# Two shared PSUM banks in turn, ScalarE's convolution steps spread out, and column sums with standing ones, in a selective-scan kernel

## The chip, the cores and the metric

The kernel runs on one core of a Trainium2 chip. The metric is the device time of one execution in microseconds (us). Each kernel was run several times in rounds, next to the kernel before on the same chip. All executions quoted here were in the fast state, and every kernel gave correct results. The kernel before had a median of 5537.85 us in the three runs that came with the case (5533.6 to 5543.78).

Names of engines: PE is TensorE, PEld its weight load, DVE is VectorE, ACT is ScalarE, POOL is GpSimd.

## The reference, cut to what matters

A binary-weight convolution block feeds a selective scan in four directions; layer norm, attention and a feed-forward layer follow. Nearly all of the time is the scan:

```python
delta = softplus(delta + delta_bias)
def step(h, inp):
    ut, dt, Bt, Ct = inp
    dA = exp(dt[..., None] * A[None])                       # decay
    h = dA * h + (dt * ut)[..., None] * Bt[:, :, None, :]   # scan
    y = einsum('bkdn,bkn->bkd', h, Ct)                      # product and sum over the state
    return (h, y)
```

There are 4 images, 4 directions, 4096 positions, 192 channels and a state of 16.

## The kernel before: the parts that matter

The scan is cut into 1536 pieces of 128 partitions by 1024 positions. Each piece needs these instructions:

- POOL "injects": `w <- dl * bc`.
- ACT makes the decay `dA` (an Exp) in one of two PSUM buffers of two banks each.
- DVE scans. Its result stays in the PSUM buffer (`dA`), or goes to SBUF (`h`) if POOL will take the product.
- DVE or POOL multiplies by C. The builder decides by running estimates: 940 products go to DVE, 596 to POOL.
- PE sums products into `yp`, a PSUM bank that holds eight pieces; ACT empties it (`ys`).
- ACT copies the last column as the carry (`cy`).

```python
for i in range(n):                     # one piece a step; cut
    if i >= 1: self.carry(i - 1)                       # ACT, one column
    if i % 8 == 3 and i > 8: self.evacuate(i - 4)      # ACT empties the bank of y
    if i + 1 < n: self.decay(i + 1)                    # ACT, Exp into a buffer "dA"
    if i >= 3: self.reduce(i - 3)                      # PE
    if i + AHEAD < n: self.inject(i + AHEAD)           # POOL
    self.late_product()                                # POOL, product of the piece before
    self.scan(i)                                       # DVE, and the product if it is DVE's
    if i % 8 == 0 and self.todo: lanes.append(self.prepare())   # delta, one tile in 8 pieces
    interleave(lanes)                                  # one step of delta
    next(back, None)                                   # one step of the "back" work
```

The "back" work is everything else (convolution, layer norms, attention, feed-forward), one step per piece. Delta is prepared in steps too; each `yield` ends a step:

```python
ps = p.ps.tile([128, 512], F32, tag="dps")             # delta's own PSUM bank
... 8 matmuls into ps ...;                         yield
ACT: Abs(ps) -> d;  ACT: Relu(ps) -> t;            yield
ACT: Exp(d) -> d;   ACT: Ln(d) -> ps;              yield
PE: ps += ident * t;                               yield
DVE: d[:, 1] = ps * u                              # "delta's product"
yield
ACT: d[:, 0] = copy(ps)                            # "delta's copy", pd <- dps
```

In the convolution, DVE forms `cz` in a PSUM bank, ACT takes its sign (`sg`) and then Exp, Ln and Exp for a SiLU, DVE makes `u` from `cz`, and ACT copies `u` by columns (`ut`) in the same step.

## Time and profile before

| What | Before | Where it is read |
|---|---|---|
| Span of the profiled run | 5538.9 us, clock 0.714 | cores |
| DVE, POOL busy | 5052.4 us, 4994.2 us (91%, 90%) | busy times |
| ACT, PE busy | 64%, 62% | busy times |
| DVE idle from 340 to 5410 us | 213 us | stretches |
| PE waits for ACT to empty y's bank | 621.9 us, 141 times | waits |
| ACT's delta copy waits for DVE | 3.7 us, once | groups |

A busy share says which engine can set the time, and its gaps say where. DVE and POOL are full; PE and ACT matter only where they make those two wait. The scans of the 1536 pieces run from about 269 to 5419 us. The lines themselves are in the prediction below.

The copy of delta is where the change bites, so here is its line in the groups of the kernel before (busy us, mean ns | idle of the engine just before it, and who ended it):

```profile
L1185 ACT COPY pd<-dps 128x512 f32<-128x512 f32 x189 | 109.2, 578 | 3.7 <-DVE pd L401 3.7
```

The 189 copies wait once, 3.7 us in all: DVE's product lies a whole step earlier.

### The profile page before, as it was taken

To read this page: it belongs to the slowest core of one execution; us is meant where nothing else is said; L and a number is where in the kernel's file an instruction comes from. 1 tells how busy PE (TensorE), PEld (TensorE's weight loads), DVE (VectorE), ACT (ScalarE), POOL (GpSimd) and SP (SyncE) were. 2 spreads that over 40 slices of the span, in tenths; PEclk is the share of its full clock that TensorE was granted. 3 is DMA by queue.
4 is the path that set the end of the run, shared out by engine and by line. 5 is a ranking of instruction groups with operands and counts; after the bars stand their busy time and mean duration, and the time that the engine had idled before them with its cause. 6 is when DMAs were issued, how large, how long until landed. Compare 5 with 4: busy or idle time off the path is not lost. (4 is left out here: it accounts for less than half of the span.)

```text
span 5538.9 us, 62371 instructions
## 1 busy us (share of the span) xinstructions
PE 3432.7 (62%) x20197; PEld 1356.7 (24%) x20197; DVE 5052.4 (91%) x3237; ACT 3556.7 (64%) x5564; POOL 4994.2 (90%) x2262
## 2 busy tenths in 40 slices
PE   6456665576557766577656766544676564444677
PEld 3222222222223222222222222211232121111223
DVE  3299999999999999899999999999999999999984
ACT  4467776777666667677766666755556775555554
POOL 2199999999999999899999999999999999999981
PEclk8667776678767876667777777766787766566778
DMA  4456666866766566666656566665666665665652
GB/s 78 118 179 198 207 194 193 258 193 199 220 203 194 194 205 199 218 217 207 205 193 212 185 200 210 212 211 191 210 215 186 191 205 198 205 208 190 207 159 60
DMA packets 613244, 1069.93 MB, mean 193 GB/s; under 512 B 225083, under 2 KB 343924, under 8 KB 611124
## 3 DMA queue, kind: packets, MB, share of 16 engines
q1 hardware_dynamic: 599428, 1065.88, 61.4%
q8 instruction: 159, 2.61, 0.2%
q10 hardware_dynamic: 13488, 0.07, 0.1%
q14 instruction: 169, 1.38, 0.1%
HBM read 833.20 MB, written 229.38 MB: 192 GB/s over the span
## 5 line engine op out<-in xcount | busy, mean ns | idle before, releaser
L401 POOL TENSOR_TENSOR w<-dl,bc 128x1024 f32<-128x1024 f32 x1536 | 3579.9, 2356 | 166.7 <-PE yp L1302 93.2
L1231 ACT ACTIVATE dA<-dl,anm 128x1024 f32<-128x1024 f32 x1536 | 1715.6, 1117 | 477.0 <-DVE w L401 291.5
L1302 PE MATMUL yp<-w,sum 128*32 128x256 f32 x12288 | 1261.6, 507 | 1083.2 <-ACT ys L1316 621.9
L401 DVE TENSOR_TENSOR_SCAN dA<-dA,cy,w 128x1024 f32<-128x1024 f32 x706 | 1654.4, 2343 | 94.7 <-ACT dA L1231 83.4
L401 POOL TENSOR_TENSOR w<-h,bc 128x1024 f32<-128x1024 f32 x596 | 1402.6, 2353 | 93.7 <-DVE h L401 85.2
L401 DVE TENSOR_TENSOR w<-dA,bc 128x1024 f32<-128x1024 f32 x940 | 1151.4, 1225 | 47.7 <-DVE dA L401 0.5
L401 DVE TENSOR_TENSOR_SCAN h<-dA,cy,w 128x1024 f32<-128x1024 f32 x446 | 1043.3, 2340 | 9.2 <-ACT dA L1231 8.7
L1302 PEld LDWEIGHTS yp<-w,sum 128*32 128x32 f32 x12288 | 308.0, 127 | 2136.9 <-issue 705.4
L1271 ACT COPY cy<-dA 128x1 f32<-128x1 f32 x707 | 110.8, 157 | 692.0 <-DVE w L401 690.7
L401 DVE TENSOR_TENSOR_SCAN dA<-dA,w 128x1024 f32<-128x1024 f32 x234 | 534.2, 2283 | 22.3 <-ACT dA L1231 18.0
L577 PE MATMUL cv<-tp,cw 96*96 96x512 fp8e5 x1152 | 359.9, 456 | 85.6 <-ACT r L627 70.5
L401 DVE TENSOR_TENSOR_SCAN h<-dA,w 128x1024 f32<-128x1024 f32 x150 | 341.8, 2279 | 24.4 <-POOL w L401 23.6
L1179 PE MATMUL dps<-sp,ident 128*128 128x512 f32 x378 | 356.8, 1043 | 0.0
L1307 PE MATMUL yp<-ya,back 128*128 128x256 f32 x576 | 237.8, 534 | 0.0
L577 PEld LDWEIGHTS <-cw 96*96 96x96 fp8e5 x1152 | 159.0, 146 | 277.5 <-issue 223.8
L1271 ACT COPY cy<-h 128x1 f32<-128x1 f32 x445 | 82.7, 186 | 145.6 <-DVE h L401 144.5
L847 PE MATMUL yc<-eys,mean 96*96 96x512 f32 x240 | 134.6, 713 | 33.3 <-DMA eys<-yd 14.5
L1307 PEld LDWEIGHTS yp<-ya,back 128*128 128x128 f32 x576 | 123.9, 248 | 127.8 <-issue 97.1
L1172 ACT ACTIVATE pd<-dps,dbias,pvd 128x512 f32<-128x512 f32 x189 | 143.8, 761 | 16.4 <-PE dps L1167 13.0
L1173 ACT ACTIVATE sp<-dps,dbias,pvd 128x512 f32<-128x512 f32 x189 | 144.7, 766 | 0.0
L401 DVE TENSOR_TENSOR pd<-dps,pu 128x512 f32<-128x512 f32 x189 | 127.6, 675 | 4.6 <-DMA dl<-dld 4.3
L1316 ACT COPY ys<-yp 128x512 f32<-128x512 f32 x192 | 111.7, 582 | 30.2 <-PE yp L1307 24.3
(282 smaller groups left out, 4017.6 us busy)
## 6 DMA issues: line engine op xcount, KB each, us to landing
dl<-dld SPq DMA_DIRECT2D x768, 512.0 KB
bc<-bcd SPq DMA_DIRECT2D x512, 512.0 KB
dld<-pd SPq DMA_DIRECT2D x126, 512.0 KB
yd<-ys SPq DMA_DIRECT2D x768, 64.0 KB
dld<-pd SPq DMA_DIRECT2D x126, 256.0 KB
ya<-yd SPq DMA_DIRECT2D x192, 128.0 KB
pu<-ud SPq DMA_DIRECT2D x32, 512.0 KB
pu<-utd SPq DMA_DIRECT2D x31, 512.0 KB
```

Source lines behind the costliest of these rows:

```text
L401: return getattr(self.eng, name)(out, *args, **kw)
L577: nc.tensor.matmul(ps, c.cw[:, j, t, 96 * h : 96 * h + 96], tpad[j][:, 8 * q + dy : 8 * q + dy + 8, dx : dx + IW], start=(j == 0 and t == ...
L847: self.c.nc.tensor.matmul(ps, w, x, start=(i == 0), stop=(i == len(pairs) - 1))
L1172: nc.scalar.activation(d[:, 0], ps, AF.Abs, scale=sc, bias=bi)
L1173: nc.scalar.activation(t, ps, AF.Relu, scale=sc, bias=bi)
L1179: nc.tensor.matmul(ps, c.ident, t, start=False, stop=True, skip_group_check=True)
L1231: c.nc.scalar.activation(t, self.dlt[i // NQ][0], AF.Exp, scale=c.anm[:, g, NQ * KORD[e] + q : NQ * KORD[e] + q + 1])
L1271: self.c.nc.scalar.copy(self.carries[g, q], h[:, CH - 1 : CH])
L1302: c.nc.tensor.matmul(y[32 * x : 32 * x + 32, g % 2, :], c.sum4, prod[:, 256 * x : 256 * x + 256], start=(q == 0), stop=(q == NQ - 1 and no ...
L1307: c.nc.tensor.matmul(y[:, g % 2, :], w, src, start=False, stop=(n == len(more) - 1))
L1316: c.nc.scalar.copy(t, y[:, :, ::-1] if k >= 2 else y)
```

## The change

The intent is to let PE start the sums of the next eight pieces while ACT still empties the last, and to even out ACT's load. The two PSUM banks that y and delta own become two banks that they use in turn, y in one and delta in the other, and they swap every eight pieces. For that, delta must be out of its bank earlier, so its copy moves into the step of DVE's product and delta starts at piece 4 of eight. The rest: the bank of y is emptied behind the decay; ACT's pairs of delta instructions are split; the store of delta is issued a step later; the sign goes to the step of `u`, `ut` a step behind `u`, and the convolution's 18 taps (its matmuls) are dealt 5, 5, 5, 3 to the steps; the column sums of x use the ones as the first, standing operand of the matmul, where x stood before; a fourth delta tile is made at the start. The diff is cut to the main lines (`...`).

```diff
-        ps = ... p.ps.tile([128, 512], F32, name=f"dps_{nm}", tag="dps")
+        ps = ... p.ps.tile([128, 512], F32, name=f"dps_{nm}", tag=f"y{1 - self.bank()}")
         nc.scalar.activation(d[:, 0], ps, AF.Abs, scale=sc, bias=bi)
+        yield
         nc.scalar.activation(t, ps, AF.Relu, scale=sc, bias=bi)
         yield
         nc.scalar.activation(d[:, 0], d[:, 0], AF.Exp, scale=-1.0)
+        yield
         nc.scalar.activation(ps, d[:, 0], AF.Ln, bias=1.0)
...
         c.vec.tensor_tensor(d[:, 1]..., ps..., uv, ALU.mult)
-        yield
         nc.scalar.copy(d[:, 0], ps)
...
-            self.ydone[i // 8] = c.p.ps.tile(..., name=f"yp_{i}", tag="y")
+            self.ydone[i // 8] = c.p.ps.tile(..., name=f"yp_{i}", tag=f"y{i // 8 % 2}")
...
+            if i + 1 < n:
+                self.decay(i + 1)
             if i % 8 == 3 and i > 8:
                 self.evacuate(i - 4)
-            if i + 1 < n:
-                self.decay(i + 1)
...
-            if i % 8 == 0 and self.todo:
+            if i % 8 == 4 and self.todo:
... (convolution, inside its steps s = 0..3)
+                    if s == 0 and turned:
+                        by_columns(*turned)          # ut, a step behind u
                         elif s == 1:
-                            ... AF.Sign of pz ...    # sg
                             nc.scalar.activation(e, pz, AF.Exp, scale=-1.0)
...
+                        elif s == 3:
+                            sign(ph, pq, pz)         # sg, now in the step of u
                             c.vec.tensor_tensor(u, pz, e, ALU.mult)
... (column sums, of 32 blocks of x)
-                nc.tensor.matmul(csum, xts[i // 8][:, i % 8, :], c.ones1, ...)
+                nc.tensor.matmul(csum, c.ones1, xts[i // 8][:, i % 8 : i % 8 + 4, :]..., ...)
```

More of the change, by code (lines that the diff above doesn't have):

```diff
@@ L188, in transposed @@
             count[0] += 1
-            ps = p.ps.tile([128, 1024], BF16, name=f"tps{count[0]}", tag=("y", "dps")[count[0] % 2])
+            ps = p.ps.tile([128, 1024], BF16, name=f"tps{count[0]}", tag=f"y{count[0] % 2}")
             at = 0
@@ L350, in weights @@
         )
-        ps = p.ps.tile([128, 512], F32, name="tpd", tag="dps")
+        ps = p.ps.tile([128, 512], F32, name="tpd", tag="y0")
         for g in range(3):
@@ L507, in prologue @@
                 yield
-            csum = bank("csum", 0)[0:96, 0:1]
-            for i in range(NT):
-                nc.tensor.matmul(csum, xts[i // 8][:, i % 8, :], c.ones1, start=(i == 0), stop=(i == NT - 1))
-                if i % 8 == 7:
-                    yield
+            csum = bank("csum", 0)[0:1, 0 : 4 * DM]
+            for i in range(0, NT, 4):
+                nc.tensor.matmul(
+                    csum, c.ones1, xts[i // 8][:, i % 8 : i % 8 + 4, :].rearrange("p i e -> p (i e)"),
+                    start=(i == 0), stop=(i == NT - 4),
+                )
+                if i % 8 == 4:
+                    yield
+            row = f32("csr")[0:1, 0 : 4 * DM]
+            nc.scalar.copy(row, csum)
+            ps = bank("cst", 1)[0:96, 0:1]
+            for i in range(4):
+                nc.tensor.matmul(
+                    ps, row[:, DM * i : DM * i + DM], c.ones1[0:1, :], start=(i == 0), stop=(i == 3)
+                )
+            yield
             cs = f32("cs")[0:96, 0:1]
-            nc.scalar.copy(cs, csum)
-            gsum = bank("gsum", 1)[0:96, 0:1]
+            nc.scalar.copy(cs, ps)
+            gsum = bank("gsum", 0)[0:96, 0:1]
             nc.tensor.matmul(gsum, c.grp, cs, start=True, stop=True)
@@ L563, in prologue, with by_columns, sign @@
             one = lambda h: slice(h, h + 1)
-            prev = None
+            prev = turned = None
             two = c.p.dA.tile([128, CH], F32, name=f"cv2_{b}", tag="dA") if alone else None
             utp = sub.enter_context(tc.tile_pool(name=f"ut_{b}", bufs=1))
+            uts = {}
+            def by_columns(h, q, u):
+                if q % 4 == 0:
+                    uts[h] = utp.tile([96, IW, 32], F32, name=f"ut{h}{q}_{b}", tag="ut")
+                ut, at = uts[h], 8 * (q % 4)
+                dst, src = ut[:, :, at : at + 8], u.rearrange("p (h w) -> p w h", w=IW)
+                (nc.gpsimd.tensor_copy if alone else nc.scalar.copy)(dst, src)
+                if q % 4 == 3:
+                    rows = slice(8 * q - 24, 8 * q + 8)
+                    c.later.store(c.utd[b][h].rearrange("p (w h) -> p w h", h=IH)[:, :, rows], ut, after=1)
+            def sign(h, q, pz):
+                sg = f32(f"sg{h}{q}")[0:96, 0:128]
+                nc.scalar.activation(
+                    sg.bitcast(F8).rearrange("p (h e i) -> p h e i", h=8, e=2),
+                    pz.rearrange("p (h i e) -> p h e i", h=8, e=2), AF.Sign, saturate=False,
+                )
+                for m in range(3):
+                    g0 = 64 * (m // 2) + 32 * h
+                    c.later.store(xgw[g0 : g0 + 32, m % 2, 128 * q : 128 * q + 128], sg[m::3, :])
             for n, part in enumerate(parts + [None]):
@@ L574, in prologue @@
                     if part:
-                        for j, t in taps[(0, 5, 9, 14)[s] : (5, 9, 14, 18)[s]]:
+                        for j, t in taps[5 * s : min(18, 5 * s + 5)]:
                             dy, dx = divmod(t, 3)
@@ L581, in prologue @@
                             )
+                    if s == 0 and turned:
+                        by_columns(*turned)
+                        turned = None
                     if prev:
@@ L587, in prologue @@
                         elif s == 1:
-                            sg = f32("sg" + pn)[0:96, 0:128]
-                            nc.scalar.activation(
-                                sg.bitcast(F8).rearrange("p (h e i) -> p h e i", h=8, e=2),
-                                pz.rearrange("p (h i e) -> p h e i", h=8, e=2), AF.Sign, saturate=False,
-                            )
-                            for m in range(3):
-                                g0 = 64 * (m // 2) + 32 * ph
-                                c.later.store(xgw[g0 : g0 + 32, m % 2, 128 * pq : 128 * pq + 128], sg[m::3, :])
+                            if alone:
+                                sign(ph, pq, pz)
                             e = f32("e" + pn)[0:96]
@@ L601, in prologue @@
                             nc.scalar.activation(e, e, AF.Exp, scale=-1.0)
-                        else:
+                        elif s == 3:
+                            if not alone:
+                                sign(ph, pq, pz)
                             u = f32("u" + pn)[0:96]
@@ L605, in prologue @@
                             c.later.store(c.ud[b][ph][:, 512 * pq : 512 * pq + 512], u)
-                            if pq % 4 == 0:
-                                ut = utp.tile([96, IW, 32], F32, name=f"ut{pn}_{b}", tag="ut")
-                            at = 8 * (pq % 4)
-                            dst, src = ut[:, :, at : at + 8], u.rearrange("p (h w) -> p w h", w=IW)
+                            turned = (ph, pq, u)
                             if alone:
-                                nc.gpsimd.tensor_copy(dst, src)
-                            else:
-                                nc.scalar.copy(dst, src)
-                            if pq % 4 == 3:
-                                rows = slice(8 * pq - 24, 8 * pq + 8)
-                                c.later.store(
-                                    c.utd[b][ph].rearrange("p (w h) -> p w h", h=IH)[:, :, rows], ut, after=1
-                                )
+                                by_columns(*turned)
+                                turned = None
                     yield
@@ L633, in prologue @@
                     yield
+            if turned:
+                by_columns(*turned)
             c.later.flush()
@@ L1119, in done, with bank @@
         return self.at > (b * NK + n) * NPC + SETTLE
+    def bank(self):
+        return max(0, self.at - 3) // 8 % 2
     def load_signs(self, b, k):
@@ L1161, in prepare @@
         d = spare[0] if spare else p.pd.tile([128, 2, 512], F32, name=f"pd_{nm}", tag="pd")
-        ps = spare[3] if spare else p.ps.tile([128, 512], F32, name=f"dps_{nm}", tag="dps")
+        ps = spare[3] if spare else p.ps.tile([128, 512], F32, name=f"dps_{nm}", tag=f"y{1 - self.bank()}")
         pv = ps.rearrange("p (c q s) -> p s q c", q=4, s=8)
@@ L1175, in prepare @@
         nc.scalar.activation(d[:, 0], d[:, 0], AF.Exp, scale=-1.0)
+        yield
         nc.scalar.activation(ps, d[:, 0], AF.Ln, bias=1.0)
@@ L1189, in prepare @@
             then = (lambda: self.loaded.add((b, k, ci, part))) if x == len(groups) - 1 else None
-            c.later.store(dst, d[r0 : r0 + n], after=1, then=then)
+            c.later.store(dst, d[r0 : r0 + n], after=2, then=then)
     def load_bc(self, w, to, b, e, ci, q):
@@ L1297, in reduce @@
         if i % 8 == 0:
-            self.ydone[i // 8] = c.p.ps.tile([128, 2, 256], F32, name=f"yp_{i}", tag="y")
+            self.ydone[i // 8] = c.p.ps.tile([128, 2, 256], F32, name=f"yp_{i}", tag=f"y{i // 8 % 2}")
         y, prod = self.ydone[i // 8], self.ins.pop(i)
@@ L1324, in run @@
         c, lanes, n = self.c, [], len(self.pieces)
-        w = [c.p.w.tile([128, CH], F32, name=f"w_s{x}", tag="w") for x in range(7)]
+        w = [c.p.w.tile([128, CH], F32, name=f"w_s{x}", tag="w") for x in range(8)]
         ps = [c.p.dA.tile([128, CH], F32, name=f"dA_s{x}", tag="dA") for x in range(2)]
@@ L1345, in run @@
             self.load_dl(m)
+        u = c.p.pu.tile([128, CH], F32, name="pu_s", tag="pu")
+        for _ in self.prepare((w[7].rearrange("p (t l) -> p t l", t=2), w[4][:, 512:CH], u, ps[1][:, 512:CH])):
+            pass
         self.decay(0)
```

## The prediction

> **What bounds the kernel now.** I read the busy times first, then busy time by stretches, then each engine's waits, then the instruction groups, and last the order of the built program.
>
> ```profile
> PE 3432.7 (62%) x20197; PEld 1356.7 (24%) x20197; DVE 5052.4 (91%) x3237; ACT 3556.7 (64%) x5564; POOL 4994.2 (90%) x2262
> 3700.00:3900.00 200.00, 97.83 (x635) 34.29 (x636) 197.48 (x115) 102.97 (x150) 196.92 (x86) 0.61 0.60 195
> 340.00:5410.00 5070.00, 3161.05 (x18864) 1214.60 (x18862) 4857.31 (x2969) 3334.33 (x5199) 4869.21 (x2120) 0.71 0.64 203
> ```
>
> The first line is the page's busy line; the others are stretches (start:end, length, busy time of PE, PEld, DVE, ACT, POOL with instruction counts, then clock and DMA). DVE and POOL share the work and are both nearly full from about 340 us, when the scans run steadily, to 5410 us. In these 5070 us DVE is idle 5070 - 4857 = 213 us and POOL 201 us. In the quietest stretch, where nothing but scans runs (3700 to 3900), DVE still idles 2.5 us of 200, or 1.3%. I take that as the floor of back-to-back issue: 1.3% of 5070 is 65 us. So at most 213 - 65, about 148 us or 2.7% of 5538, can come out of the steady part by any reordering, unless work is removed.
>
> ```profile
> L401 POOL TENSOR_TENSOR w<-dl,bc 128x1024 f32<-128x1024 f32 x1536 | 3579.9, 2356 | 166.7 <-PE yp L1302 93.2 <-DMA dl<-dld 62.8 <-DMA bc<-bcd 7.4
> L401 POOL TENSOR_TENSOR w<-h,bc 128x1024 f32<-128x1024 f32 x596 | 1402.6, 2353 | 93.7 <-DVE h L401 85.2 <-DMA x1b<-x1d 1.5 <-PE yp L1307 1.4
> L401 DVE TENSOR_TENSOR_SCAN dA<-dA,cy,w 128x1024 f32<-128x1024 f32 x706 | 1654.4, 2343 | 94.7 <-ACT dA L1231 83.4 <-ACT cy L1271 7.2 <-POOL w L401 2.7
> L1316 ACT COPY ys<-yp 128x512 f32<-128x512 f32 x192 | 111.7, 582 | 30.2 <-PE yp L1307 24.3 <-PE yp L1302 5.0 <-DMA dl<-dld 0.6
> ```
>
> These are groups: line, engine, operation, shapes, count, then busy us and mean ns of one, then idle before them and who ended it. None of POOL's 1536 + 596 multiplications goes away: in the order of the built programs POOL again has 1536 and 596, and DVE 1536 scans and 940 products. What can shrink is the right-hand column.
>
> ```profile
> PE yp L1302 <- ACT ys L1316: 621.9, 141, 10.8
> DVE dA L401 <- ACT dA L1231: 101.3, 86, 5.5
> POOL w L401 <- PE yp L1302: 93.6, 58, 8.6
> ACT ut L614 <- DVE u L401: 91.6, 45, 3.6
> DVE g L401 <- PE sy L847: 19.7, 9, 4.6
> ```
>
> In these lines of the waits (total, times, longest) the largest, 622 us, belongs to PE, which is 62% busy: it is the wait that two banks are to remove, but it counts only where it ends in one of the two small ones below it, PE making POOL wait (93.6) and ACT making DVE wait (101.3). The two small ones add, since DVE and POOL feed each other over a few buffers; POOL's 85 us on DVE's h are the echo of DVE's own stalls.
>
> **What the Trainium skill says.** "Perfetto Trace Analysis", Identifying the Most-Contended Engine, says to work on the engine with the highest occupancy and find what its gaps wait for. The trace agrees: PE's 622 us lie on an engine with room, DVE and POOL are the ones to look at. "PSUM — Partial Sum Buffer", PSUM bank collisions raise a hardware error, says two engines must not touch one bank in the same quadrant at once, reads against reads included, and that software has to keep them apart. The trace fits: ScalarE's one-column carry copy, which only needs the scan, mostly starts after DVE's product from the same tile (waits of ACT cy on DVE w: 690.7 us). [...]"ScalarE: Activation LUTs", Rules for kernel authors, budgets about 0.3 us per activation plus 0.83 ns per element, 0.73 us for 512. The trace has 0.58 to 0.77, so splitting ScalarE's steps moves work without making it cheaper.
>
> **Two banks in turn.** Before, y has one bank and delta the other. The first sum of an eight-piece block waits until ScalarE has emptied the bank. Afterwards it goes to the other bank; but delta now lives there for most of the block. In the built program the first sum of a block waits for ScalarE's copy of delta, which stands at the end of the step after DVE's delta product. Before: wait for scan (and product) of piece i+2, carry 0.16, copy 0.58. After: the same scan, delta product 0.68, copy 0.58, so about 0.5 us later. So the 622 us wait of PE is mostly not removed: it gets a new name. What improves is the tie to a late PE: the evacuation no longer stands between PE's last sum and its next, and the delta matmul that needs it comes two sums later. Of POOL's 93.6 us on PE, the five longest (8.6, 5.65, 5.12, 3.58, 3.02, sum 26) come after PE stood on a DMA (delta's signs, the x load of the column sums) and stay. Of the other 68, mostly in the epilogue where PE is 75% busy, I expect a third or so to go: -25 us.
>
> **Evacuation behind the decay.** ScalarE waited 24.3 + 5.0 us for PE in front of its evacuation, with the next decay behind it; and in about eight places delta's Exp and Ln, another pair and the evacuation lined up ahead of one decay, some 2 us late each. Not all of it reached DVE: -10 us.
>
> **Delta's copy in the same step as DVE's product.** ScalarE now stands on DVE at that place. Afterwards it has copy 0.5, up to 1.3 of other work, carry 0.1 and decay 1.05 before DVE's next scan but one; DVE has a scan of 2.29, and a product of 1.15 if it is its own. Walking the built order with these durations, 32 of the 188 places come late, 0.27 us each on average: +9 us.
>
> **Decays that wait for the scan right before their own.** In the built program most decays wait for the piece two back, but 73 of 1536 wait for the previous scan (on a tile whose product POOL takes); after the change it is 87. Each such decay (1.12 us) can't hide, and the trace shows DVE gaps of exactly 1.25 us, 48 us in 46 gaps over 0.3 us. 14 more, of which 46/73 count: 14 x 0.63 x 1.25 = +11 us.
>
> **Convolution, u a step behind.** ACT's 91.6 us on u go, but ACT has room there: between 1200 and 1400 us, a convolution, DVE is busy 98.63 and 97.03 of each 100 us, near the floor of 98.7. About 1 us per 100 over three convolutions of some 260 us: at most -6, say -5 us. ScalarE's total per part is unchanged.
>
> **Column sums.** Before, 32 matmuls (64 passes) with a weight load each, 10.3 us a batch at the start, 2.7 us a step later. After, 8 matmuls of 384 columns, 16 passes; the trace's 512-column fp32 passes take 0.56 to 1.04 us, so 384 take 0.4 to 0.8 by estimate, 7 to 12 us. A wash, plus one copy and four tiny matmuls. The stall there (DVE busy 89.00 of 100 at 1000 to 1100) starts with PE waiting for x from DMA and stays: -3 us in all.
>
> **Start.** A fourth delta tile is made before the first scan. ScalarE and PE have the time (they wait for dl until 264.9), but DVE's product needs a u load issued at 264.33 behind six dl loads; DMA is busy until about 273.7, and the first scan began at 268.96. Up to 5 us late, but POOL fills its six tiles until 280.4 and DVE waits 9.2 us for it anyway; and one delta step less at once. +2 us. The rest of the start and the tail are the same work.
>
> Sum: -25 - 10 + 9 + 11 - 5 - 3 + 2 = -21 us; 5538 - 21 = 5517 us.
>
> **Rivals.** First, PE's idle time is the real brake: epilogue and prologue matmuls stand in order behind the blocked sum, ScalarE stands behind them (sq on yc 78.5, fq on fc 42.4 us) and DVE behind ScalarE. For it: DVE is busy only 195.8 of the last 230 us before 5410. Against: much of that is PE's own load. It could bring 70 to 90 us: 5450 to 5470. Second, the new ties cost more than they free: the bank comes back only after DVE's delta product, so a late DVE blocks PE, PE blocks POOL, and ScalarE standing on DVE delays back work and decays. Against: POOL fills four pieces ahead with nine tiles, so a sum may be about two pieces (6.6 us) late. It could cost 30 to 50 us: 5570 to 5590. Third, all gaps of DMA origin stay and nothing moves: 5538.
>
> **Range and chances.** The terms are some 10 to 25 us each with the first the least sure. 5455 to 5570 holds both half-strength rivals. Faster by over 2% means below 5427, 111 of the 148 us that are there at all: 0.04. Slower by 2%, above 5648, would need a new stall at every block (0.6 us at each of 188): 0.03. Same: 0.93.
>
> **What would show it.** PE's wait for ACT ys nearly gone and a wait for ACT pd of a few hundred us in its place; POOL's wait on PE near 70; DVE's wait on ACT dA between 95 and 120; ACT's wait on u gone and one on DVE pd new; busy time of POOL and DVE unchanged. If POOL's wait on PE falls below 30 us, or DVE's wait on ACT rises above 150, I was wrong.

## The result, and the profile after

The changed kernel took 5578.6 us (median of four runs, 5574.11 to 5580.39) against 5539.91 us for the kernel before in the same rounds: 39 us slower. The ratio is 1.007, with a 95% interval of 1.0052 to 1.0087. Ratios here are the mean time of one kernel's fast runs over that of the other's of the same rounds, so not quite the ratio of the medians quoted. The prediction, 5517 us with a range of 5455 to 5570, had the sign wrong and missed the range. "Same within 2%" was right.

Busy times of the changed kernel, from its page, and then its stretches (start:end, length, busy time of PE, PEld, DVE, ACT, POOL with counts, clock, DMA share, GB/s):

```profile
PE 3522.2 (63%) x20037; PEld 1360.0 (24%) x20037; DVE 5054.6 (91%) x3237; ACT 3546.4 (64%) x5568; POOL 4995.2 (90%) x2262
```

```profile
3700.00:3900.00 200.00, 96.64 (x630) 33.25 (x630) 197.50 (x113) 104.01 (x152) 197.22 (x86) 0.65 0.58 190
340.00:5410.00 5070.00, 3217.35 (x18556) 1209.21 (x18556) 4830.94 (x2950) 3301.92 (x5171) 4845.72 (x2109) 0.70 0.64 202
```

DVE and POOL do the same work to within about 2 us. In the quiet stretch, where scans and delta run without back work, DVE is busy 197.50 us of 200, as before. In the long stretch its idle time rose from 213 to 239 us. So the loss is more waiting, and it lies where back work runs beside the scans and delta.

The groups of the changed kernel that answer to those shown of before, and the copy:

```profile
L401 POOL TENSOR_TENSOR w<-dl,bc 128x1024 f32<-128x1024 f32 x1536 | 3578.8, 2355 | 156.9 <-PE yp L1333 77.5 <-DMA dl<-dld 68.2 <-DMA bc<-bcd 5.8
L401 POOL TENSOR_TENSOR w<-h,bc 128x1024 f32<-128x1024 f32 x596 | 1402.3, 2353 | 137.3 <-DVE h L401 123.2 <-PE yp L1338 3.0 <-DMA yd<-ys 1.9
L401 DVE TENSOR_TENSOR_SCAN dA<-dA,cy,w 128x1024 f32<-128x1024 f32 x705 | 1651.8, 2343 | 94.0 <-ACT dA L1262 73.2 <-ACT cy L1302 8.8 <-POOL w L401 6.3
L1216 ACT COPY pd<-dps 128x512 f32<-128x512 f32 x188 | 110.0, 585 | 459.3 <-DVE pd L401 459.3
```

And its waits (who waits for whom: us in total, times, longest):

```profile
PE yp L1333 <- ACT pd L1216: 358.3, 104, 6.4
POOL w L401 <- PE yp L1333: 77.5, 48, 6.6
DVE dA L401 <- ACT dA L1262: 96.7, 80, 2.8
DVE u L401 <- ACT sg L594: 12.6, 14, 2.2
DVE dA L401 <- ACT cy L1302: 11.3, 8, 2.5
DVE pd L401 <- PE dps L1211: 10.2, 3, 7.5
```

Each line that the prediction named came about as named: the wait of PE is renamed from `ys` to `pd`; POOL's wait on PE fell from 93.6 to 77.5; DVE's wait on the decay, here 96.7, stayed in its band. The copy, which waited 3.7 us before, now stands 459.3 us on DVE (184 times), and this costs ACT nothing that its own busy time would show. By itself such a stand need not cost DVE anything. In the quiet stretch (3700 to 3900 us) the copy waits as well, in eight places, and DVE has no gap there that the waits show (over 0.15 us):

```profile
ACT pd L1216 <- DVE pd L401: 19.5, 8, 3.1
```

Elsewhere new small lines stand against DVE: 12.6 us on the sign, 10.2 us on delta's own matmul, more on carries.

To account for it, I summed DVE's gaps from the 32nd scan to the last in both traces. That stretch is 38.6 us longer after the change, and DVE's idle time in it grew by 36.5 us (212.4 to 248.9). By who ended the gap: sign +12.6, PE for delta's product +10.2, carries +5.4, PE for the attention sums (`vk`) +5.0, PE for the output (`op`) +4.3, decays +4.3, POOL +4.2, column sums +2.8; against these PE's `sy` -6.5 and a late DMA of delta's -4.3. Note how little of it is decays, 4.3 us, although the prediction's two terms on late decays came to 20; the evacuation, moved by the same change, may be one reason (experiment evac_only).

### The profile page after: what moved, and what is told of

It reads as the page before. It is cut to its first block, busy times and chain, and to the rows that moved or that the text cites. A ratio compares the mean times of both kernels' runs of the same rounds, so it can differ in the third digit from the quotient of the medians.

```text
span 5572.3 us, 61825 instructions
## 1 busy us (share of the span) xinstructions
PE 3522.2 (63%) x20037; PEld 1360.0 (24%) x20037; DVE 5054.6 (91%) x3237; ACT 3546.4 (64%) x5568; POOL 4995.2 (90%) x2262
## 5 line engine op out<-in xcount | busy, mean ns | idle before, releaser
L401 POOL TENSOR_TENSOR w<-dl,bc 128x1024 f32<-128x1024 f32 x1536 | 3578.8, 2355 | 156.9 <-PE yp L1333 77.5
L1333 PE MATMUL yp<-w,sum 128*32 128x256 f32 x12288 | 1328.6, 528 | 827.8 <-ACT pd L1216 358.3
L1216 ACT COPY pd<-dps 128x512 f32<-128x512 f32 x188 | 110.0, 585 | 459.3 <-DVE pd L401 459.3
L1338 PE MATMUL yp<-ya,back 128*128 128x256 f32 x576 | 216.4, 493 | 0.0
L1211 PEld LDWEIGHTS dps<-sp,ident 128*128 128x128 f32 x376 | 85.9, 284 | 384.8 <-ACT dps L1208 325.6
L1197 PE MATMUL dps<-gT,wdz 128*128 128x64 fp8e5 x1000 | 119.8, 323 | 37.9 <-DMA gT<-gTd 20.0
```

Source lines behind the costliest of these rows:

```text
L401: return getattr(self.eng, name)(out, *args, **kw)
L1197: nc.tensor.matmul(pv[:, s], wd[:, k, s], gT[:, :, c0 : c0 + 16], start=(s == 0), stop=(s == 7))
L1211: nc.tensor.matmul(ps, c.ident, t, start=False, stop=True, skip_group_check=True)
L1216: nc.scalar.copy(d[:, 0], ps)
L1333: c.nc.tensor.matmul(y[32 * x : 32 * x + 32, g % 2, :], c.sum4, prod[:, 256 * x : 256 * x + 256], start=(q == 0), stop=(q == NQ - 1 and no ...
L1338: c.nc.tensor.matmul(y[:, g % 2, :], w, src, start=False, stop=(n == len(more) - 1))
```

## The experiments

Eighteen kernels were run, each in five rounds beside the kernel before. In the first four expectations, theory A is that the sign stands in DVE's way in the convolution and the banks cost the rest; theory B is that the banks cost all of it. The next ones set "ACT's copy of delta stands on DVE" against "PE gets its bank back late".

### 1. Which part costs

**conv_only**: the kernel before with the convolution's hunks alone (sign to the step of `u`, `ut` a step behind, taps 5, 5, 5, 3).

```diff
-                        for j, t in taps[(0, 5, 9, 14)[s] : (5, 9, 14, 18)[s]]:
+                        for j, t in taps[5 * s : min(18, 5 * s + 5)]:
...
-                            sg = ...; nc.scalar.activation(sg..., pz..., AF.Sign)   # at s == 1
+                            sign(ph, pq, pz)                                        # at s == 3, ahead of u
...
-                                nc.scalar.copy(dst, src)                            # ut, at s == 3
+                        by_columns(*turned)                                         # ut, at s == 0 of the next
```

> Only the convolution's part on the kernel before: sign moved to the step of u, taps 5,5,5,3, u turned a step behind. Theory A (the moved sign reads the bank of cz just where DVE's u has to read it): 10 to 20 us slower than before, DVE waiting for ACT sg at u some 12 to 16 us. Theory B (the banks cost all of the 39 us): same as before within 6 us, or a little faster, since ACT's 92 us on u are gone.

Measured 5547.09 us against 5536.98: ratio 1.0016 (1.0009 to 1.0023), so 10 us slower, as theory A said. But DVE's wait for the sign is smaller than the 12 to 16 us that it named:

```profile
DVE u L401 <- ACT sg L582: 5.2, 5, 1.7
```

So about half of these 10 us is the sign; the rest is not accounted for, beyond a few microseconds more behind carries and decays.

**banks_only**: the two banks, delta's new steps, the fourth start tile and the evacuation behind the decay, without convolution and column sums.

```diff
-        ps = ... tag="dps")                 # delta
+        ps = ... tag=f"y{1 - self.bank()}")
-            self.ydone[i // 8] = ... tag="y")
+            self.ydone[i // 8] = ... tag=f"y{i // 8 % 2}")
... (with delta's new steps, start and copy, and the evacuation, as in the change above)
```

> Only the two banks with the shifted delta steps, the fourth start tile and the evacuation behind the decay; convolution and column sums as before. Theory A: 15 to 25 us slower, the rest lies in the convolution. Theory B: 35 to 40 us slower, PE on ACT pd some 350 us, DVE pd on PE some 10 us. If the prediction's own sum for these parts held (-25-10+9+11+2) it would be 13 us faster.

Measured 5557.13 us: ratio 1.0037 (1.0024 to 1.0049), 20 us slower. PE's wait for the copy of delta:

```profile
PE yp L1307 <- ACT pd L1190: 294.3, 94, 6.3
```

**no_conv**: the changed kernel with the convolution's hunks undone: the diff of conv_only, read backwards.

> The changed kernel with the convolution as before; differs from banks_only by the column sums alone. Theory A: 12 to 20 us faster than the changed kernel, that is 20 to 27 us slower than before. Theory B: as slow as the changed kernel (+39 us). The column sums: within 5 us of banks_only.

Measured 5563.05 us: ratio 1.0047 (1.0033 to 1.0061), 26 us slower.

**sign_back**: the changed kernel with the sign back in the step of Exp.

```diff
                         elif s == 1:
-                            if alone:
-                                sign(ph, pq, pz)
+                            sign(ph, pq, pz)
...
-                            if not alone:
-                                sign(ph, pq, pz)
```

> The changed kernel with only the sign put back beside the Exp one step after cz, everything else kept. Theory A: DVE's wait at u for ACT sg (12.6 us) gone and 10 to 16 us faster than the changed kernel. Theory B, or if it is the turned u or the taps that cost: within 5 us of the changed kernel.

Measured 5568.94 us: ratio 1.0053 (1.004 to 1.0065), so some 10 us of the loss seems to go. The interval still overlaps that of the changed kernel (1.0052 to 1.0087), which was timed in other rounds.

**evac_only**, the evacuation behind the decay alone, and **csum_only**, the column sums alone:

```diff
+            if i + 1 < n:
+                self.decay(i + 1)
             if i % 8 == 3 and i > 8:
                 self.evacuate(i - 4)
-            if i + 1 < n:
-                self.decay(i + 1)
```

```diff
-            for i in range(NT):
-                nc.tensor.matmul(csum, xts[i // 8][:, i % 8, :], c.ones1, ...)
+            for i in range(0, NT, 4):
+                nc.tensor.matmul(csum, c.ones1, xts[i // 8][:, i % 8 : i % 8 + 4, :]..., ...)
... (then one copy of the row and four small matmuls that turn it)
```

> The kernel before with only the evacuation of y moved behind the next decay. By the prediction's term 10 us faster; with the walk of the built order (94.6 us of late decays before, 89.5 here) 5 us faster. If the evacuation's place is itself part of what makes the two banks slow (PE must now wait one decay, about 1 us, longer for the only bank), 5 us or more slower. I expect within 5 us of before.

> The kernel before with only the column sums taken with standing ones. If the 6 us between no_conv and banks_only are real: 4 to 8 us slower than before, from the longer chain of copies (one copy of the row, four small matmuls) in front of the sign of x in three batches. If they are the noise of another instruction order: within 3 us of before.

Measured 5538.03 us (ratio 1.0002, 0.9994 to 1.001) and 5543.38 us (1.0008, 1.0001 to 1.0014), against 5538.56. The evacuation's place is worth nothing in sum; the column sums cost about 5 us. In evac_only's trace the nothing is a balance. DVE's wait on decays fell from 101.3 us, as the prediction had it, but POOL's wait on PE rose from 93.6, and DVE now waits for PE before delta's product, which it did not before:

```profile
DVE dA L401 <- ACT dA L1231: 86.6, 74, 5.2
POOL w L401 <- PE yp L1302: 113.3, 79, 8.8
DVE pd L401 <- PE dps L1179: 15.6, 15, 3.9
```

What follows: every part but the evacuation loses, and the parts nearly add up: banks +20, convolution +10, column sums +5 make +35 of the 39. The banks are the largest. Here is how the sign does its part, from the timeline of the changed kernel (start, duration, engine, instruction, in brackets the idle time before it and who ended it):

```profile
630.60 1.12 ACT L1262 ACTIVATE dA<-dl,anm 128x1024 f32<-128x1024 f32 x1 [0.38 <-DVE h L401]
631.66 0.58 ACT L1347 COPY ys<-yp 128x512 f32<-128x512 f32 x1
632.13 0.59 ACT L594 ACTIVATE sg<-cz 96x512 fp8e5<-96x512 f32 x1
...
632.75 0.69 DVE L401 TENSOR_TENSOR u<-cz,e 96x512 f32<-96x512 f32 x1 [2.19 <-ACT sg L594]
```

Sign and `u` only read `cz`, and `u` uses nothing of the sign. Yet `u` waits for the sign here: the two reads of one PSUM bank are kept apart, in the order in which they were written, as the rule that the prediction cites would have it. DVE stood 2.19 us until ACT had got round to the sign, behind a decay and an evacuation.

### 2. Late return of the bank, or the copy's place

**banks_short**: banks_only with Abs and Relu in one step again, Exp and Ln too, and a `yield` between DVE's product and the copy, so that the bank comes back a step earlier than in banks_only.

```diff
         nc.scalar.activation(d[:, 0], ps, AF.Abs, scale=sc, bias=bi)
-        yield
         nc.scalar.activation(t, ps, AF.Relu, scale=sc, bias=bi)
         yield
         nc.scalar.activation(d[:, 0], d[:, 0], AF.Exp, scale=-1.0)
-        yield
         nc.scalar.activation(ps, d[:, 0], AF.Ln, bias=1.0)
...
             uv, ALU.mult
         )
+        yield
         nc.scalar.copy(d[:, 0], ps)
```

> banks_only with ScalarE's pairs (Abs and Relu, Exp and Ln) in one step as before the change and the copy one step behind DVE's product: delta leaves its bank at step 17 of the block count instead of 18, with a sum wanting it at 19, and ScalarE no longer stands on DVE. If delta's late, DVE-bound copy is what makes the banks slow: 15 to 30 us faster than banks_only, that is from 5 us slower to 10 us faster than before; PE's wait on ACT pd below 100 us; ACT's wait for DVE pd (454 us) below 50. If it is the turn-taking itself: as slow as banks_only (+20 us).

Measured 5541.25 us: ratio 1.0007 (0.9999 to 1.0015), 16 us faster than banks_only. PE's wait for the copy is 94.6 us and ACT's wait for DVE's product 0.7, all as expected if the copy is what costs.

**banks_start3**: banks_only with delta started at piece 3 of eight and the `yield` before the copy; the bank comes back at the same piece as in banks_only.

```diff
-            if i % 8 == 4 and self.todo:
+            if i % 8 == 3 and self.todo:
...
             uv, ALU.mult
         )
+        yield
         nc.scalar.copy(d[:, 0], ps)
```

> banks_only with the same six ScalarE steps, but delta begun one piece earlier (piece 3 of 8) and the copy one step behind DVE's product, so the bank comes back at the same step as in banks_only. ScalarE no longer stands on DVE (454 us of ACT on DVE pd gone, late decays by the walk 93 in place of 130 us), PE's wait on ACT pd stays at 250 to 350 us. If ScalarE's stand on DVE is the cause: 15 to 20 us faster than banks_only. If the late return of the bank to the sums is: as slow as banks_only.

Measured 5523.57 us (5515.97 to 5526.73): ratio 0.997 (0.9961 to 0.998). This is 34 us faster than banks_only and faster than before. Its waits:

```profile
PE yp L1308 <- ACT pd L1191: 335.8, 108, 7.9
POOL w L401 <- PE yp L1308: 67.0, 38, 5.3
```

PE waits for the copy 335.8 us here, more than the 294.3 of banks_only, and the kernel is faster. So the late return of the bank is not what costs these 34 us. And POOL's wait on PE, 93.6 us before, is down by 27, which is what the two banks were to bring. How much of the drop is theirs stays open: the next kernel, with the banks untouched, has 78.9.

### 3. The copy by itself, both repairs, short steps again

**before_copy_same**: the kernel before, banks untouched, only the `yield` before the copy removed.

```diff
             uv, ALU.mult
         )
-        yield
         nc.scalar.copy(d[:, 0], ps)
```

> The kernel before, banks untouched, with one thing changed: ScalarE copies delta in the same step in which DVE forms delta's product, instead of a step later. If ScalarE standing in its own order behind DVE's product is by itself what cost banks_only 34 us against banks_start3: 10 to 20 us slower than before (fewer than the 34, since here the bank is returned to nobody else's sums), a line of ScalarE's copy waiting for DVE's product of 300 us or more in the waits, and DVE idle behind decays up by 10 us or more. If the copy costs only together with the turn of the two banks or with the earlier start: within 5 us of before.

Measured 5550.03 us against 5536.35: ratio 1.0025 (1.0016 to 1.0034), 14 us slower. The line of the copy in its groups:

```profile
L1184 ACT COPY pd<-dps 128x512 f32<-128x512 f32 x189 | 110.5, 585 | 407.1 <-DVE pd L401 407.1
```

Time and wait came as expected; the rise of DVE's wait on decays (106.8 to 107.6 us) did not. What rose were carries (11.8 to 16.3). This trace can't tell where the 14 us went, though: its execution took 5541.12 us, the fastest of eleven (the others 5548.3 to 5555.86), and DVE idles only 5 us more in it than in the trace of the kernel before.

**start3**: the changed kernel with the edit of banks_start3. **after_mended**: the same, and the sign back as in sign_back.

> The changed kernel with the first repair alone: delta copied a step after DVE's product, sign change left in the step of u. If the sign in the step of u costs what conv_only showed: 5 to 10 us slower than after_mended, with DVE's wait of u for ScalarE's sign change of 8 us or more in the trace. If the sign's wait is hidden once ScalarE no longer stands in the copy: within 3 us of after_mended.

> The changed kernel with two repairs: the copy of delta a step after DVE's product (delta started one piece earlier, so the bank comes back at the same piece) and the sign change back in its own step. If both costs found so far are separate and add up: banks_start3 (15 us faster than before), plus the convolution's spread without its sign (0 to +4), plus column sums (0 to +6): 5525 to 5535, that is 5 to 15 us faster than before and 40 to 50 faster than the changed kernel. If the changed kernel loses its time in something else that the two repairs leave in place (column sums, the turn of u a step behind): 5545 to 5565.

Measured 5509.83 us for start3 (ratio 0.9953, 0.994 to 0.9965) and 5508.0 us for after_mended (5502.08 to 5512.67; 0.9945, 0.9932 to 0.9957). after_mended beats the kernel before by 28 us and the changed kernel by 71, more than I expected. The sign, left where the change put it, costs nothing clear of noise once the copy is repaired: the medians lie 2 us apart, the intervals overlap, and DVE's wait for it fell to 3.3 us. In the groups of start3 the copy waits for nothing and `u` nearly nothing for the sign:

```profile
L1217 ACT COPY pd<-dps 128x512 f32<-128x512 f32 x188 | 108.6, 578 | 0.1
L401 DVE TENSOR_TENSOR u<-cz,e 96x512 f32<-96x512 f32 x64 | 43.5, 680 | 43.5 <-ACT e L633 37.3 <-ACT sg L594 3.3 <-DMA xg<-sg 2.5
```

**banks_short3**: banks_start3 with the short steps of banks_short (the first two `yield`s of that diff taken out).

> banks_start3 with delta's short steps put together again (Abs with Relu, Exp with Ln), so that the bank comes back one or two pieces earlier. If the late return of the bank (PE waiting for the copy) costs nothing in the end: within 8 us of banks_start3, though PE's wait for the copy falls from 336 us to under 150. If the return matters: 10 us or more faster than banks_start3. If two elementwise passes in one step hold up a decay: slower than banks_start3 by 10 or more, like banks_short (5541).

Measured 5559.34 us: ratio 1.0035 (1.0023 to 1.0048), 36 us slower than banks_start3 though the bank comes back earlier still. DVE's gaps behind decays are the same in both (109.1 us); the waits show a new one, 1.8 us in banks_start3:

```profile
DVE pd L401 <- PE dps L1183: 25.6, 12, 5.9
```

With the short steps, delta's product often comes before PE has done delta's matmul, and DVE stands on it. Splitting ACT's pairs, a part of the change that I had counted as neutral, seems to be worth something here.

### 4. One yield, and a hidden variable

Two doubts were left. banks_start3 had changed two things at once, the start and the copy. And the builder's choice of who takes a product depends on its own running estimates: of the 596 products on POOL, half are other pieces after the change than before. So I split the two edits, and dealt the products out anew.

**banks_s3_same** and **after_s3_same**: banks_only and the changed kernel, started at piece 3, the copy still in the step of the product.

```diff
-            if i % 8 == 4 and self.todo:
+            if i % 8 == 3 and self.todo:
```

> banks_only with delta started one piece earlier and nothing else: ScalarE's copy still in the step of DVE's product. If the copy standing on DVE is the cause: 5545 to 5560, like banks_only, with ScalarE's copy waiting for DVE's product for over 300 us. If the earlier start (an earlier return of the bank) is the cause: 5520 to 5530, like banks_start3.

> The changed kernel with delta started one piece earlier and nothing else. If the copy standing on DVE is the cause of the loss: 5560 to 5580. If the start is: 5505 to 5525, like start3. If each does half: 5535 to 5550.

Measured 5588.13 us (ratio 1.009, 1.0076 to 1.0104) and 5584.96 us (1.0084, 1.007 to 1.0097), both slower than even the first theory's ranges (to 5560 and 5580). The earlier start gains nothing by itself; it even loses. Against banks_start3 and start3, from which they differ in one `yield`, they are 65 and 75 us slower. DVE's waits, first banks_s3_same, then after_s3_same, and start3 last:

```profile
DVE dA L401 <- ACT dA L1236: 145.0, 95, 7.8
DVE h L401 <- ACT dA L1236: 17.0, 10, 4.7
```

```profile
DVE dA L401 <- ACT dA L1262: 113.8, 88, 4.4
DVE h L401 <- ACT dA L1262: 26.4, 9, 5.4
DVE u L401 <- ACT sg L594: 13.9, 12, 2.4
```

```profile
DVE dA L401 <- ACT dA L1263: 80.4, 63, 3.2
DVE h L401 <- ACT dA L1263: 19.2, 8, 4.8
```

**before_shift**, **after_shift**, **mended_shift**, **short3_shift**: the kernel before, the changed kernel, after_mended and banks_short3 with another threshold for the deal of products.

```diff
-        pool = c.vec.us + 1.2 > c.gps.us + 2.4
+        pool = c.vec.us + 1.7 > c.gps.us + 2.4
```

> The kernel before with the threshold of the builder's choice raised by 0.5 us, so that 206 of some 596 products on POOL go to other pieces; no instruction is added or removed but one product. If the deal of products is harmless: within 5 us of before. If it is a hidden variable of the size of the differences here: 10 us or more to either side.

> The changed kernel with the same new threshold (216 of 596 products on other pieces). If the loss of 39 us belongs to the change itself: within 10 us of the changed kernel, 5568 to 5588. If it belongs to the deal of products: 15 us or more nearer to before, 5560 or less.

> after_mended with the same new threshold. If the gain of 28 us on before belongs to the repairs: 5500 to 5518. If it is a lucky deal: 5525 or more. The difference to after_shift, with nearly the same deal, should again be 50 us or more if the repairs are what counts.

> banks_short3 with the threshold of the builder's choice raised by 0.5 us, so that 210 of 596 products on POOL go to other pieces. If delta's short steps from the earlier start cost by themselves: within 8 us of banks_short3 (5559). If banks_short3 had an unlucky deal: 5525 to 5545.

| Kernel | Ratio to before | With the new deal |
|---|---|---|
| before | 1 | 0.9992 (5534.97 us) |
| changed | 1.007 | 1.0059 (5570.65 us) |
| after_mended | 0.9945 | 0.9961 (5514.82 us) |
| banks_short3 | 1.0035 | 1.0043 (5565.43 us) |

A new deal moved these kernels by 8 us at most. after_mended stays 56 us ahead of the changed kernel with nearly the same deal. And in the built programs the pairs that differ in one `yield` alone (before and before_copy_same, banks_start3 and banks_s3_same, start3 and after_s3_same) have the very same pieces on POOL, so the deal has no part in their 14, 65 and 75 us. Differences of 5 us between kernels of other deals, such as the column sums' cost, are within what the deal alone can do, and I claim no more of them.

### How the copy does its harm

Here is one place in the timeline of the changed kernel, during the projection work (`tbc`, `sgn`) at 825 us:

```profile
823.25 1.22 DVE L401 TENSOR_TENSOR w<-dA,bc 128x1024 f32<-128x1024 f32 x1
824.39 0.68 DVE L401 TENSOR_TENSOR pd<-dps,pu 128x512 f32<-128x512 f32 x1
824.99 2.34 DVE L401 TENSOR_TENSOR_SCAN h<-dA,cy,w 128x1024 f32<-128x1024 f32 x1
825.10 0.59 ACT L1216 COPY pd<-dps 128x512 f32<-128x512 f32 x1 [2.88 <-DVE pd L401]
825.59 0.78 ACT L711 ACTIVATE tbc<-acc,sbR 128x512 f32<-128x512 f32 x1
...
826.26 0.78 ACT L712 ACTIVATE sgn<-acc,sbR 128x512 fp8e5<-128x512 f32 x1
...
826.92 0.17 ACT L1302 COPY cy<-dA 128x1 f32<-128x1 f32 x1
...
827.36 1.12 ACT L1262 ACTIVATE dA<-dl,anm 128x1024 f32<-128x1024 f32 x1 [0.28 <-DVE h L401]
...
828.58 2.36 DVE L401 TENSOR_TENSOR_SCAN dA<-dA,cy,w 128x1024 f32<-128x1024 f32 x1 [1.25 <-ACT dA L1262]
```

ACT idles 2.88 us in front of the copy, with two back instructions and the carry `cy` of piece 162 queued behind it. Then it waits again, for the scan of piece 163 (`h`), before it may make the decay of piece 164. DVE has nothing to do meanwhile and loses 1.25 us, the whole decay (1.12 us) and the hand-over.

Why should the decay of piece 164 wait for the scan of piece 163? The addresses in the built program tell: the decays of pieces 162, 163, 164 lie in PSUM banks 2, 0, 0. Normally the two buffers alternate, and a decay waits for the piece two back. Here piece 162's buffer was still held by its late carry, while piece 163, whose scan writes to SBUF because POOL takes its product, gave up its buffer at the scan's end. So the decay was given the buffer just freed, and could no longer be made ahead. That the builder hands out the buffer that is free first is my inference from these addresses; I have not read its rule.

Counting such decays in the built programs, and in the traces the gaps (over 0.2 us, from about the 32nd scan on) in front of their scans, the nth scan being piece n, gives this (sums to about 1 us):

| Kernel | Copy | Decays on the buffer just freed | of these behind a copy of delta | DVE's gaps before all of these | DVE's gaps before those behind a copy |
|---|---|---|---|---|---|
| before | a step later | 73 | 5 | 72.4 us | 2.5 us |
| before_copy_same | same step | 88 | 24 | 76.7 us | 14.9 us |
| banks_only | same step | 88 | 20 | 93.3 us | 21.9 us |
| banks_s3_same | same step | 100 | 26 | 111.1 us | 19.1 us |
| banks_start3 | a step later | 75 | 3 | 84.3 us | 3.8 us |
| changed | same step | 87 | 29 | 82.8 us | 28.9 us |
| after_s3_same | same step | 87 | 21 | 93.2 us | 16.3 us |
| start3 | a step later | 61 | 6 | 63.5 us | 6.3 us |
| after_mended | a step later | 66 | 6 | 63.7 us | 6.3 us |

Between after_s3_same and start3, one `yield` apart, the stretch from the 32nd scan to the last is 70.5 us longer and DVE idles 64.0 us more in it. Decays account for 40.6 of these (29.7 of them on buffers just freed), the sign for 10.6, the issue of instructions for about 5, POOL for 4.8 and carries for 3.9. So decays on buffers just freed are the largest single item, but not the only one: whatever ACT has to do for DVE can come later when ACT stands on DVE first. The table is a count and not an experiment. No run held the buffers fixed, only 10 of the 29.7 us lie right behind a copy, and between before and before_copy_same the sum rose by 4.3 us only (in that fast execution).

## Why the prediction was wrong, point by point

The sum was -21 us and the change brought +39, so it was off by 60. The banks' part was put at -13 (-25 - 10 + 9 + 11 + 2) and measured +20 (banks_only), 33 us off; the convolution is 15 off (-5, measured +10), and the column sums 8 (-3, measured +5). With the copy a step later the banks' part comes to -15 (banks_start3). So the copy accounts for the 33 us, and it is the step of the prediction that failed: it was put at +9 and costs 34 there (banks_only against banks_start3), and 69 in the changed kernel (against start3).

- **What bounds the kernel**: right. DVE and POOL kept their busy times and their quiet floor; all that moved was DVE's idle time in stretches with other work. PE's longest wait was only a name, as said.
- **Two banks in turn, -25**: PE's wait got a new name, as said. POOL's wait on PE fell by 16 us in the changed kernel and by 27 in banks_start3, which is 15 us faster than before. Kernels with the banks untouched range from 78.9 (before_copy_same) to 113.3 (evac_only), so the drop of 16 is not shown to be the banks'; no run tried the banks alone. The reading of the five longest waits was not exact: waits of 4.2 and 3.2 us were passed over. The Trainium skill ("Perfetto Trace Analysis", Matmuls) advises to rotate matmul groups through PSUM banks so that evacuation overlaps; here PE's sums no longer wait for the evacuation (621.9 us before), but for delta in the other bank (358.3 us).
- **Evacuation behind the decay, -10**: no effect in sum (evac_only, ratio 1.0002). The gain on decays came (DVE's wait 15 us less), but the term left out that the bank comes free later (PE's wait for it rose from 621.9 to 798.5 us): POOL's wait on PE rose by 20 us, and DVE's for PE before delta's product by 15.6.
- **Delta's copy in the same step as DVE's product, +9**: this is the step that failed, by its size. The mechanism was named, and 32 late places were counted, close to the 31 gaps behind decays that the trace shows 3.3 to 7 us after a copy (5 such gaps before). These gaps are 33.5 us, 1.1 us each where I had 0.27; 27 of the 31 decays sit on the buffer just freed, where a decay loses its whole length. Not all of it is new, as DVE's gaps behind all decays rose by 4.3 us only. And I followed only decays: sign, carries and back work stand behind the copy as well. By itself the edit cost 14 us in the kernel before, 34 with the banks in turn and the bank back at the same piece, and 65 to 75 us at an equal start at piece 3.
- **Decays that wait for the scan right before their own, +11**: near in size. The gaps before them grew from 72.4 to 82.8 us. (The reading behind it, 48 us in 46 gaps, left out seven longer gaps of 20 us together.) But I had taken it as a separate accident of the build. The counts tie it to the copy: 29 of them lie behind a copy after the change and 5 before, and the others became fewer.
- **Convolution, -5**: wrong by itself (+10), and the step that failed was that ACT's work there only moves. In the step of `u` the sign shares a bank with DVE's read and stands in front of it: 12.6 us in the changed kernel, 5.2 in conv_only, where the other half of the 10 us stays open. With the copy repaired it is harmless, and start3, with spread convolution and column sums, is not behind banks_start3 (ratio 0.9953 against 0.997).
- **Column sums, -3**: measured +5, with an interval that barely leaves zero and a size that a new deal of products can make. **Start, +2**: not separable; the first scans of the profiled runs lie up to 12 us apart.
- **The rivals**: the second one happened, its size ("30 to 50 us: 5570 to 5590") included (the stated range ended just where it began), and its last clause, ScalarE standing on DVE, was the part that counted; its first, the bank coming back late, was not. I gave it too little room because I set the terms +9 and -25 against each other as if both were equally sure.
- **The citations**: the advice to find what an engine's gaps wait for stands in the page's next section, Optimization Strategy; and the 0.73 us for 512 elements was an estimate worked from the figures of "ScalarE: Activation LUTs", for which the trace has 0.58 to 0.77.
- **The alarms**: I had set them on single lines (POOL on PE below 30, DVE on the decay above 150). None went off, since the loss spread over the sign, carries, and delta's product. The sum of all DVE gaps would have told.

What stays open: why the earlier start without the `yield` loses another 31 us in banks_s3_same but 6 in after_s3_same, and how much of the cost would go if the decays were tied to two fixed buffers in turn. The last would test the inference on buffers directly, and the runs were used up. Open too: whether the banks alone, without delta's new steps, gain anything.

## What to carry to other kernels

When two engines read one PSUM bank, and the second has other work queued behind its read for which the first will wait, put a step of other work between the two reads: here ACT, standing in its own order on DVE, passed its delay on to carries and decays that DVE needed, though its own busy share showed nothing. Where there was no back work, as in the quiet stretch, the same stand cost nothing. When buffers are handed out as they come free, check in the built program which instructions get the buffer that was freed last, for such a decay could no longer run ahead here. And judge a change of order by the sum of the bound engine's gaps, with a control that shuffles the build, since here a shuffle alone moved up to 8 us.

## What the Trainium skill lacked or had wrong

- "PSUM — Partial Sum Buffer", PSUM bank collisions raise a hardware error, gives the rule that two engines' accesses to a bank must be kept apart, reads included, and the traces agree with it. It gives no price. Here the one read of delta's bank that followed in the same step stood 459.3 us on DVE, and moving it one step apart was worth 65 to 75 us of 5585 with the banks in turn, and 14 us of 5550 in the kernel before.
- "Perfetto Trace Analysis", Identifying the Most-Contended Engine, points to the engine with the highest occupancy. That led to DVE rightly, but occupancy did not tell the kernels apart: DVE's busy time is 5054.6 us in the changed kernel and 5047.5 in after_mended, which is 71 us faster. What told them apart were DVE's gaps (64.0 us between after_s3_same and start3), to which the page's next section does send the reader; the cause lay in the order on ACT, at 64%.
- No page that I read tells that a two-buffer pool can give successive tiles the same buffer, or what that costs: 87 of 1536 decays in the changed kernel, with gaps of DVE of typically 1.25 us, where the alternating order hides the decay (61 in start3).
